# Three F32R products in place of one F32 product in the down-projections of a GNN and expert-FFN kernel

## The chip, the core and the metric

The kernel runs on one core of a Trainium2 chip. A core has five engines that work at the same time, each with a queue of its own that it takes in order: TensorE (PE, with its weight loads shown apart as PEld), VectorE (DVE), ScalarE (ACT), GpSimd (POOL) and SyncE (SP, which here only starts transfers). Matrix products are written to PSUM, which has eight banks of 512 float32 columns on 128 partitions; VectorE and ScalarE read them from there. The metric is the device time of one execution in microseconds (us).

## The reference, cut to what matters

1250 rows of 1024 features pass through four residual layers: a graph attention layer, a wide feed-forward layer with random "rails", a graph convolution, and a mixture of experts. All of it is float32. The change lies in the last layer, whose hidden width is 256:

```python
def geglu(x, w1, w2, w3):
    return jax.nn.gelu(x @ w1, approximate=False) * (x @ w2) @ w3
...
shared = geglu(xf, w1s, w2s, w3s)
idx = jnp.argmax(xf @ Wg, axis=-1)
for e in range(8):
    y = geglu(xf, W1[e], W2[e], W3[e])
    final = final + jnp.where((idx == e)[:, None], y, 0.0)
return x + shared + final
```

The down-projection is the product with w3: [rows, 256] by [256, 1024], once for all rows (shared) and once for each expert on its own rows.

## The kernel before, in words

The first 2460 us of the execution (attention, the wide layer as a blocked fast matrix product, and the graph convolution) hold no edit. The graph convolution ends with a gather (`gather`, L1088 to L1092): counts in F32R times rows that were split into a rounded part and the rest, both F32R, two matmuls each in place of one F32 matmul.

The last layer begins with `hidden` (L1158) for the shared projection: for each half f of the 256 hidden columns and each of three chunks of rows, two groups of eight matmuls (L1166) into the PSUM tiles pab0 and pab1, then a gelu on ScalarE (L1171) and a product on VectorE (L1172). Beside it POOL sends out the row numbers of each expert and gathers the first expert's rows.

Then the shared down-projection: ten tiles t of 125 rows, each with four F32 products (two f, two halves g of the 1024 outputs, L1280), two adds into X on VectorE (L1286) and a write of the tile to base_d by SP (L1287). During the last four tiles, `turn_rows(0)` transposes the first expert's gathered rows on PE (L1269), copied out in turn by VectorE and ScalarE (L1272). After it SP writes all tiles of X to the output (L1289).

Then eight experts, each with room for 224 rows (CAP), in two parts of 128 and 96. `hidden` computes four groups of sixteen matmul rows, and after each group takes one of the four turns of `turn_rows(e + 1)`, the transposes for the next expert. The down-projection has, for each part s and half g, two F32 products into po6 (L1302) and an add on VectorE (L1305) to rows that were gathered from base_d (`rows_of`, L1255); when both halves are done, POOL scatters the part's rows to the output (L1306).

PSUM is shared out so: pool ab has pab0 and pab1 twice (four banks), tps has two banks for transposes, ops6 has po6 twice. w12, w3t, xgT and hid are each held twice, xg and base three times.

The order on each engine's queue and the moment at which a buffer is reused are settled when the program is built: the builder takes instructions by their place in the program and by durations that it estimates, so that loads and gathers can stand far ahead of their place in the text. Each engine then waits on semaphores for what it needs. An F32 matmul in the program appears as two matmul rows in the profile, an F32R matmul as one.

Of the kernel before, what the change touches and what calls it, by code (L numbers as in the profile page):

```python
# [102 lines left out]
def gnn_ffn_kernel(ctx, tc, x, src, dst, gat_w, a_l, a_r, maker, up, cproj,  # L103
# [543 lines left out]
    with nullcontext(ctx) as tail:  # L647
        low = tail.enter_context(tc.tile_pool(name="lowp", bufs=1)).tile([P, T * D], F32, name="low")
# [383 lines left out]
        def weights3(w3t, c):  # L1032
            nc.sync.dma_start(w3t, c.rearrange("(k p) o -> p k o", p=P))
            return w3t
# [116 lines left out]
    with back_end:  # L1151
        hsp = back_end.enter_context(tc.tile_pool(name="hsp", bufs=1))
        hs, w3sh = hsp.tile([P, 2, N], F32, name="hs"), weights3(hsp.tile([P, 2, D], F32, name="w3s"), w3s)
        gp = back_end.enter_context(tc.tile_pool(name="gp", bufs=3))
        with tc.tile_pool(name="ab", bufs=2, space=PSUM) as abp, tc.tile_pool(name="tps", bufs=2, space=PSUM) as tps, \
                tc.tile_pool(name="ops6", bufs=2, space=PSUM) as ops:

            def hidden(dst, w12, rhs, cols, then=None, turns=()):  # L1158
                turns = iter(turns)
                for f in range(2):  # L1160
                    for n0, nn in cols:
# [10 lines left out]
                        nc.vector.tensor_tensor(dst[:, f, n0:n0 + nn], ps[1][:, :nn], g[:, :nn], op=ALU.mult)  # L1172
# [72 lines left out]
            hidden(hs, w12s, xT5, NCH, then=places)  # L1245
# [3 lines left out]
            with tc.tile_pool(name="w12", bufs=2, side="right") as w12p, tc.tile_pool(name="xg", bufs=3) as xgp, \  # L1249
                    tc.tile_pool(name="w3p", bufs=2) as w3p, tc.tile_pool(name="xgT", bufs=2) as xgTp, \  # L1250
                    tc.tile_pool(name="hp", bufs=2) as hp, tc.tile_pool(name="yp", bufs=3, side="right") as yp:
# [6 lines left out]

                xgTs = {}
                out_t = out.rearrange("(t p) d -> t p d", p=R)  # L1260

                def turn_rows(e):
                    xgTs[e] = xgTp.tile([P, KD, CAP], F32, name="xgT")
                    for s, m in parts:
                        xg = rows_of(xn_d, s, m, e * (ROWS // P) + s, "xg")
                        for g in range(2):
# [4 lines left out]
                            eng = nc.scalar.copy if g else nc.vector.tensor_copy  # L1271
                            eng(xgTs[e][:, 4 * g:4 * g + 4, s * P:s * P + m], pt[:, :, :m])  # L1272
# [3 lines left out]
                for t in range(T):  # L1276
                    pos = [abp.tile([P, 512], F32, name=f"pab{g}") for g in range(2)]
                    for f in range(2):
                        for g in range(2):
                            nc.tensor.matmul(pos[g][:R], hs[:, f, t * R:(t + 1) * R], w3sh[:, f, g * 512:(g + 1) * 512],  # L1280
                                             start=(f == 0), stop=(f == 1))
                    if t >= T - 4:
                        next(turns, None)
                    for g in range(2):
                        xs = X[:, t, g * 512:(g + 1) * 512]
                        nc.vector.tensor_tensor(xs, pos[g][:R], xs, op=ALU.add)  # L1286
                    dma(nc.sync, base_d[t * R:(t + 1) * R, :], X[:, t, :])  # L1287
# [3 lines left out]
                for e in range(NE):  # L1291
                    w12 = weights12(w12p.tile([P, 2, KD, F], F32, name="w12"), w1[e], w2[e])
                    w3t = weights3(w3p.tile([P, 2, D], F32, name="w3t"), w3[e])
                    hid = hp.tile([P, 2, CAP], F32, name="hid")
                    hidden(hid, w12, xgTs[e], [(0, CAP)], turns=turn_rows(e + 1) if e + 1 < NE else ())
                    for s, m in parts:
                        i = e * (ROWS // P) + s
                        y = rows_of(base_d, s, m, i, "base")
                        for g in range(2):
                            po = ops.tile([P, 512], F32, name="po6")  # L1300
                            for f in range(2):
                                nc.tensor.matmul(po[:m], hid[:, f, s * P:s * P + m],  # L1302
                                                 w3t[:, f, g * 512:(g + 1) * 512], start=(f == 0), stop=(f == 1))
                            ys = y[:m, g * 512:(g + 1) * 512]
                            nc.vector.tensor_tensor(ys, po[:m], ys, op=ALU.add)  # L1305
# [4 lines left out]
                        tc.add_to_no_dep_group("rows", put.ins)  # L1310

# [80 lines left out]
```

## Time and profile before

| | us |
|---|---|
| median of three runs | 2744.56 (2742.64 to 2751.24) |
| the profiled execution's own time | 2747.47 |
| its span, first to last instruction | 2745.7 |
| PE busy | 2709.5 (99%) |
| DVE busy | 1579.3 (58%) |
| ACT busy | 906.2 (33%) |
| mean granted clock of TensorE | 0.997 |
| shared hidden products | about 2471 to 2540 |
| shared down-projection | about 2540 to 2575 |
| the eight experts | about 2575 to 2740 |

A row of a group gives the line in the kernel, the engine, the operation, the tensors (output, arrow, inputs), the shapes (output, arrow, inputs), the number of instructions, then after the bar the busy time and the mean duration in ns, and after the second bar the idle time ahead of them on that engine and what ended it. A row of the timeline or the chain begins with the start time and the duration, both in us. "PE po L1302 x16" is sixteen matmuls of line 1302 that write the tile po.

### The profile page before, as it was taken

To read this page: it belongs to the slowest core of one execution; us is meant where nothing else is said; L and a number is where in the kernel's file an instruction comes from. 1 tells how busy PE (TensorE), PEld (TensorE's weight loads), DVE (VectorE), ACT (ScalarE), POOL (GpSimd) and SP (SyncE) were. 2 spreads that over 40 slices of the span, in tenths; PEclk is the share of its full clock that TensorE was granted. 3 is DMA by queue.
4 is the path that set the end of the run, shared out by engine and by line. 5 is a ranking of instruction groups with operands and counts; after the bars stand their busy time and mean duration, and the time that the engine had idled before them with its cause. 6 is when DMAs were issued, how large, how long until landed. Compare 5 with 4: busy or idle time off the path is not lost. (4 is left out here: it accounts for less than half of the span.)

```text
span 2745.7 us, 32205 instructions
## 1 busy us (share of the span) xinstructions
PE 2709.5 (99%) x11189; PEld 1893.0 (69%) x11189; DVE 1579.3 (58%) x2708; ACT 906.2 (33%) x1611; POOL 775.8 (28%) x1016
## 2 busy tenths in 40 slices
PE   8999999999999999999999999999999999999998
PEld 6678886676676666766667667666676754675676
DVE  9668988564646556645655556455546765431322
ACT  2333345434434344344343443443432011210000
POOL 2000001243443434434344334343442110112131
PEclk9999999999999999999999999999999999999999
DMA  6336216499999999999999999999998540452784
GB/s 186 92 84 180 71 39 228 164 201 172 210 205 177 227 182 199 199 166 189 190 159 204 179 173 197 166 192 182 143 227 228 169 92 0 87 119 63 270 298 157
DMA packets 269147, 457.74 MB, mean 167 GB/s; under 512 B 53672, under 2 KB 143952, under 8 KB 268593
## 3 DMA queue, kind: packets, MB, share of 16 engines
q0 software_dynamic: 126896, 278.80, 58.7%
q1 hardware_dynamic: 142072, 176.67, 21.4%
q8 instruction: 97, 1.59, 0.2%
q14 instruction: 82, 0.67, 0.1%
HBM read 180.57 MB, written 277.02 MB: 167 GB/s over the span
## 5 line engine op out<-in xcount | busy, mean ns | idle before, releaser
L735 POOL DMA_DIRECT2D acc_d<-low x686 | 589.7, 860 | 914.4 <-ACT low L731 894.1
L731 ACT COPY low<-po 128x626 f32<-128x626 f32 x735 | 501.0, 682 | 952.8 <-PE po L722 891.8
L722 PE MATMUL po<-X,arena 128*128 128x313 f32 x2208 | 619.4, 427 | 0.0
L722 PEld LDWEIGHTS po<-X,arena 128*128 128x128 f32 x2208 | 415.2, 189 | 175.6 <-ACT low L731 16.0
L722 PE MATMUL po<-low,arena 128*128 128x313 f32 x1520 | 429.7, 428 | 0.0
L722 PEld LDWEIGHTS po<-low,arena 128*128 128x128 f32 x1520 | 285.5, 189 | 121.4 <-ACT low L731 11.6
L722 PE MATMUL po<-X,first_w 128*128 128x313 f32 x776 | 222.1, 428 | 1.8 <-DVE X L715 1.8
L722 PE MATMUL po<-X,BZ 128*128 128x313 f32 x720 | 208.5, 433 | 3.6 <-DVE BZ L715 3.6
L722 PEld LDWEIGHTS po<-X,first_w 128*128 128x128 f32 x776 | 145.7, 190 | 64.7 <-ACT low L731 7.6
L722 PE MATMUL po<-low,first_w 128*128 128x313 f32 x624 | 179.5, 429 | 1.0 <-DVE low L715 1.0
L722 PEld LDWEIGHTS po<-X,BZ 128*128 128x128 f32 x720 | 136.9, 192 | 62.6 <-issue 6.1
L722 PEld LDWEIGHTS po<-low,first_w 128*128 128x128 f32 x624 | 117.9, 190 | 50.8 <-ACT low L731 4.4
L227 PE MATMUL pz<-W,xT 128*125 128x256 f32 (+1 forms) x480 | 142.0, 455 | 0.3 <-ACT xT L160 0.3
L715 DVE TENSOR_TENSOR X<-X 128x626 f32<-128x626 f32 x125 | 101.2, 813 | 67.1 <-PE po L722 58.9
L722 PE MATMUL po<-low,BZ 128*128 128x313 f32 x480 | 137.6, 427 | 0.0
L715 DVE TENSOR_TENSOR arena<-arena 128x512 f32<-128x512 f32 x126 | 86.3, 687 | 65.6 <-PE po L722 63.1
L227 PEld LDWEIGHTS pz<-W,xT 128*125 128x125 f32 x480 | 90.0, 190 | 43.8 <-issue 33.8
L715 DVE TENSOR_TENSOR X<-X,low 128x626 f32<-128x626 f32 x105 | 85.3, 816 | 56.2 <-PE po L722 46.0
L722 PEld LDWEIGHTS po<-low,BZ 128*128 128x128 f32 x480 | 90.1, 189 | 38.2 <-ACT low L731 3.7
L715 DVE TENSOR_TENSOR X<-low,X 128x626 f32<-128x626 f32 x101 | 81.7, 813 | 53.3 <-PE po L722 49.0
L707 ACT ACTIVATE X<-pz 128x626 f32<-128x626 f32 (+8 forms) x220 | 101.6, 524 | 17.9 <-PE pz L537 17.9
L715 DVE TENSOR_TENSOR low<-X 128x626 f32<-128x626 f32 x100 | 80.9, 811 | 38.3 <-PE po L722 31.1
(304 smaller groups left out, 3383.6 us busy)
## 6 DMA issues: line engine op xcount, KB each, us to landing
acc_d<-low POOLq DMA_DIRECT2D x735, 313.0 KB, 6.2
arena<-in_cproj SPq DMA_DIRECT2D x148, 256.0 KB
w<-in_w SPq DMA_DIRECT2D x16, 1024.0 KB
BZ<-in_cproj SPq DMA_DIRECT2D x56, 256.0 KB
first_w<-in_cproj SPq DMA_DIRECT2D x52, 256.0 KB
w3t<-in_w SPq DMA_DIRECT2D x8, 1024.0 KB
low<-acc_d SPq DMA_DIRECT2D x19, 313.0 KB
X<-acc_d SPq DMA_DIRECT2D x19, 313.0 KB
```

The lines of the kernel that those rows point to most:

```text
L227: made_z = nc.tensor.matmul(pz, xT[:, k, t * R:(t + 1) * R], W[hs[0] // 2][:, k, i:i + len(hs)], start=(k == 0), stop=(k == KD - 1))
L707: nc.scalar.activation(view(key)[:, :, n0 - n * NQ:n1 - n * NQ], pz[:, 2 * i:2 * i + 2, a + n0 - c0:a + n1 - c0], AF.Gelu)
L715: tt(view(k), *a, op=ALU.add if sign == "+" else ALU.subtract)
L722: nc.tensor.matmul(po[:, o, :NQ], view(x)[:, q, o * P:(o + 1) * P], view(y)[:, q, :], start=(i == q == 0), stop=(i + 1 == len(pairs) and q ...
L731: nc.scalar.copy(part, po[:, :, :NQ])
L735: sent[:] = [nc.gpsimd.dma_start(out=acc_d[p - 1, i - 1], in_=part, accum_op=ALU.add).ins]
```

## The change

It replaces the F32 products of the experts' down-projection, and those of eight of the ten shared tiles, by three F32R matmuls each. Each operand is split into a top part T of 12 bits and the rest l. The stationary ("fixed") operand keeps T, L = 4096 l and S = l - T/4096; the moving operand keeps T, L = l and S = T - 4096 l. Two matmuls add T T and L L into one bank, the third puts S S into a second bank, and the first bank times (1 + 1/4096) plus the second is the product T T + T l + l T + l l. So each result of 512 columns takes two banks, and VectorE adds it in two instructions (`add_sums`).

The parts are made by ScalarE and VectorE: three instructions for each half of a weight matrix (`parts_moving`), four for each half of the hidden columns (`parts_fixed`). Shared tiles 0 and 1 stay F32 products, and the shared weights are split after each of them. An expert's weights are split during its own hidden products, after the first and second group.

The parts of weights and hidden columns lie in the buffer of `low`, which held the transposed rows of the shared projection; the hidden columns of the shared tiles get buffers of their own. w3t is held once instead of twice and is shared with the shared weights, hid once instead of twice. PSUM keeps eight banks: pairs of banks come two out of three times from pool ab and the third time from pool ops6, which now has one pair (`pair_of_sums`).

In an expert the three products of f=0 run for three of the four (s, g) halves, then the last of the four turns, which moves here from the end of `hidden`, then f=1 half by half with its add, and then the fourth half with both f. The copies of transposed rows all go to ScalarE. The gather of base rows now stands in the text with the add, after the products.

Left out of the diff below: the branch for experts with more than 224 rows, which isn't taken here (it makes its transposed rows anew, since `low` is overwritten).

```diff
@@ -1150,12 +1151,44 @@
-        hs, w3sh = hsp.tile([P, 2, N], F32, name="hs"), weights3(hsp.tile([P, 2, D], F32, name="w3s"), w3s)
-        gp = back_end.enter_context(tc.tile_pool(name="gp", bufs=3))
+        w3p = back_end.enter_context(tc.tile_pool(name="w3p", bufs=1))
+        hs, w3sh = hsp.tile([P, 2, 417], F32, name="hs"), weights3(w3p.tile([P, 2, D], F32, name="w3t"), w3s)
+        gp = back_end.enter_context(tc.tile_pool(name="gp", bufs=2))
-                tc.tile_pool(name="ops6", bufs=2, space=PSUM) as ops:
+                tc.tile_pool(name="ops6", bufs=1, space=PSUM) as ops:
...
+            def parts_moving(top, mix, low_part, x):
+                nc.scalar.activation(top, x, AF.Copy, scale=1.0 - 2.0 ** -13)
+                nc.vector.tensor_tensor(low_part, x, top, op=ALU.subtract)
+                nc.vector.scalar_tensor_tensor(mix, low_part, -4096.0, top, op0=ALU.mult, op1=ALU.add)
+
+            def parts_fixed(top, mix, low_part, x):
+                nc.scalar.activation(top, x, AF.Copy, scale=1.0 - 2.0 ** -13)
+                nc.vector.tensor_tensor(low_part, x, top, op=ALU.subtract)
+                nc.vector.scalar_tensor_tensor(mix, top, -(2.0 ** -12), low_part, op0=ALU.mult, op1=ALU.add)
+                nc.scalar.activation(low_part, low_part, AF.Copy, scale=4096.0)
+
+            pairs = [0]
+
+            def pair_of_sums():
+                pairs[0] += 1
+                if pairs[0] % 3 == 0:
+                    return [ops.tile([P, 512], F32, name=f"po{i}") for i in range(2)]
+                return [abp.tile([P, 512], F32, name=f"pab{i}") for i in range(2)]
+
+            def three_products(po, m, f, fixed, moving):
+                (ft, fs, fl), (mt, ms, ml) = fixed, moving
+                for i, (a, b) in enumerate(((ft, mt), (fl, ml))):
+                    nc.tensor.matmul(po[0][:m], a, b, start=(f == i == 0), stop=(f == i == 1))
+                nc.tensor.matmul(po[1][:m], fs, ms, start=(f == 0), stop=(f == 1))
+
+            def add_sums(dst, po, m):
+                nc.vector.scalar_tensor_tensor(dst, po[0][:m], 1.0 + 2.0 ** -12, dst, op0=ALU.mult, op1=ALU.add)
+                nc.vector.tensor_tensor(dst, po[1][:m], dst, op=ALU.add)
...
@@ -1169,7 +1202,9 @@
                         g = gp.tile([P, 417], F32, name="g")
                         nc.scalar.activation(g[:, :nn], ps[0][:, :nn], AF.Gelu)
-                        nc.vector.tensor_tensor(dst[:, f, n0:n0 + nn], ps[1][:, :nn], g[:, :nn], op=ALU.mult)
+                        h = dst(f, n0, nn)
+                        nc.vector.tensor_tensor(h, ps[1][:, :nn], g[:, :nn], op=ALU.mult)
+                        split(f, n0, nn, h)
...
@@ -1242,13 +1277,19 @@
-            hidden(hs, w12s, xT5, NCH, then=places)
+            HK = 2 * R
+            hsT, hsS, hsL = (hsp.tile([P, 2, N - HK], F32R, name=f"hs{i}") for i in "TSL")
+
+            def split_shared(f, n0, nn, x):
+                c0 = max(n0, HK)
+                parts_fixed(*(v[:, f, c0 - HK:n0 + nn - HK] for v in (hsT, hsS, hsL)), x[:, c0 - n0:])
+
+            hidden(lambda f, n0, nn: gp.tile([P, 417], F32, name="h", bufs=2)[:, :nn] if n0 else hs[:, f],
+                   w12s, xT5, NCH, then=places, split=split_shared)
...
-            with tc.tile_pool(name="w12", bufs=2, side="right") as w12p, tc.tile_pool(name="xg", bufs=3) as xgp, \
-                    tc.tile_pool(name="w3p", bufs=2) as w3p, tc.tile_pool(name="xgT", bufs=2) as xgTp, \
-                    tc.tile_pool(name="hp", bufs=2) as hp, tc.tile_pool(name="yp", bufs=3, side="right") as yp:
+            with tc.tile_pool(name="w12", bufs=2, side="right") as w12p, tc.tile_pool(name="xg", bufs=3) as xgp, tc.tile_pool(name="xgT", bufs=2) as xgTp, tc.tile_pool(name="xgT", bufs=2) as xgTp:
...
+                again = lowp.tile([P, T * D], F32R, name="low")
+                w3T, w3S, w3L = (again[:, i * 2 * D:(i + 1) * 2 * D].rearrange("p (f o) -> p f o", f=2) for i in range(3))
+                hidT, hidS, hidL = (again[:, 6 * D + i * 2 * CAP:][:, :2 * CAP].rearrange("p (f n) -> p f n", f=2)
+                                    for i in range(3))
+                hid = xgp.tile([P, 2, CAP], F32, name="hid", bufs=1)
@@ -1268,22 +1315,32 @@
-                            eng = nc.scalar.copy if g else nc.vector.tensor_copy
-                            eng(xgTs[e][:, 4 * g:4 * g + 4, s * P:s * P + m], pt[:, :, :m])
+                            nc.scalar.copy(xgTs[e][:, 4 * g:4 * g + 4, s * P:s * P + m], pt[:, :, :m])
                             yield
...
                 turns = turn_rows(0)
                 for t in range(T):
-                    pos = [abp.tile([P, 512], F32, name=f"pab{g}") for g in range(2)]
-                    for f in range(2):
+                    if t < 2:
+                        pos = [abp.tile([P, 512], F32, name=f"pab{g}") for g in range(2)]
+                        for f in range(2):
+                            for g in range(2):
+                                nc.tensor.matmul(pos[g][:R], hs[:, f, t * R:(t + 1) * R],
+                                                 w3sh[:, f, g * 512:(g + 1) * 512], start=(f == 0), stop=(f == 1))
                         for g in range(2):
-                            nc.tensor.matmul(pos[g][:R], hs[:, f, t * R:(t + 1) * R], w3sh[:, f, g * 512:(g + 1) * 512],
-                                             start=(f == 0), stop=(f == 1))
+                            xs = X[:, t, g * 512:(g + 1) * 512]
+                            nc.vector.tensor_tensor(xs, pos[g][:R], xs, op=ALU.add)
+                        parts_moving(w3T[:, t], w3S[:, t], w3L[:, t], w3sh[:, t])
+                    else:
+                        at = slice(t * R - HK, (t + 1) * R - HK)
+                        pos = [pair_of_sums() for _ in range(2)]
+                        for f in range(2):
+                            for g in range(2):
+                                ws = [w[:, f, g * 512:(g + 1) * 512] for w in (w3T, w3S, w3L)]
+                                three_products(pos[g], R, f, [h[:, f, at] for h in (hsT, hsS, hsL)], ws)
+                        for g in range(2):
+                            add_sums(X[:, t, g * 512:(g + 1) * 512], pos[g], R)
                     if t >= T - 4:
                         next(turns, None)
-                    for g in range(2):
-                        xs = X[:, t, g * 512:(g + 1) * 512]
-                        nc.vector.tensor_tensor(xs, pos[g][:R], xs, op=ALU.add)
                     dma(nc.sync, base_d[t * R:(t + 1) * R, :], X[:, t, :])
@@ -1291,23 +1348,50 @@
                 for e in range(NE):
                     w12 = weights12(w12p.tile([P, 2, KD, F], F32, name="w12"), w1[e], w2[e])
                     w3t = weights3(w3p.tile([P, 2, D], F32, name="w3t"), w3[e])
-                    hid = hp.tile([P, 2, CAP], F32, name="hid")
-                    hidden(hid, w12, xgTs[e], [(0, CAP)], turns=turn_rows(e + 1) if e + 1 < NE else ())
-                    for s, m in parts:
+                    turns = turn_rows(e + 1) if e + 1 < NE else iter(())
+
+                    def beside():
+                        for i in range(4):
+                            if i < 3:
+                                next(turns, None)
+                            if i < 2:
+                                parts_moving(w3T[:, i], w3S[:, i], w3L[:, i], w3t[:, i])
+                            yield
+
+                    hidden(lambda f, n0, nn: hid[:, f], w12, xgTs[e], [(0, CAP)], turns=beside(),
+                           split=lambda f, n0, nn, x: parts_fixed(hidT[:, f], hidS[:, f], hidL[:, f], x))
+                    halves = [(s, m, g, pair_of_sums()) for s, m in parts for g in range(2)]
+
+                    def multiply(halves, f):
+                        for s, m, g, po in halves:
+                            at, to = slice(s * P, s * P + m), slice(g * 512, (g + 1) * 512)
+                            three_products(po, m, f, [h[:, f, at] for h in (hidT, hidS, hidL)],
+                                           [w[:, f, to] for w in (w3T, w3S, w3L)])
+
+                    ys = {}
+
+                    def add_rows(s, m, g, po):
                         i = e * (ROWS // P) + s
-                        y = rows_of(base_d, s, m, i, "base")
-                        for g in range(2):
-                            po = ops.tile([P, 512], F32, name="po6")
-                            for f in range(2):
-                                nc.tensor.matmul(po[:m], hid[:, f, s * P:s * P + m],
-                                                 w3t[:, f, g * 512:(g + 1) * 512], start=(f == 0), stop=(f == 1))
-                            ys = y[:m, g * 512:(g + 1) * 512]
-                            nc.vector.tensor_tensor(ys, po[:m], ys, op=ALU.add)
+                        if g == 0:
+                            ys[s] = rows_of(base_d, s, m, i, "base")
+                        add_sums(ys[s][:m, g * 512:(g + 1) * 512], po, m)
+                        return g and put_rows(m, i, ys[s])
+
+                    def put_rows(m, i, y):
                         put = nc.gpsimd.indirect_dma_start(
                             out=out, out_offset=bass.IndirectOffsetOnAxis(ap=tok[:m, i:i + 1], axis=0),
                             in_=y[:m], in_offset=None, bounds_check=N - 1, oob_is_err=False)
                         tc.declare_no_dep(put.ins, group="rows", reason="rows of their own")
                         tc.add_to_no_dep_group("rows", put.ins)
+
+                    multiply(halves[:3], 0)
+                    next(turns, None)
+                    for h in halves[:3]:
+                        multiply([h], 1)
+                        add_rows(*h)
+                    multiply(halves[3:], 0)
+                    multiply(halves[3:], 1)
+                    add_rows(*halves[3])
 
         with tc.tile_pool(name="ops7", bufs=2, space=PSUM) as ops:
             def project(w3t, h, t, dst):
```

More of the change, by code (lines that the diff above doesn't have):

```diff
@@ L647, in gnn_ffn_kernel @@
     with nullcontext(ctx) as tail:
-        low = tail.enter_context(tc.tile_pool(name="lowp", bufs=1)).tile([P, T * D], F32, name="low")
+        lowp = tail.enter_context(tc.tile_pool(name="lowp", bufs=1))
+        low = lowp.tile([P, T * D], F32, name="low")
         Hs = low[:R].rearrange("p (t d) -> p t d", d=D)
@@ L1155, in gnn_ffn_kernel @@
         with tc.tile_pool(name="ab", bufs=2, space=PSUM) as abp, tc.tile_pool(name="tps", bufs=2, space=PSUM) as tps, \
-                tc.tile_pool(name="ops6", bufs=2, space=PSUM) as ops:
-            def hidden(dst, w12, rhs, cols, then=None, turns=()):
+                tc.tile_pool(name="ops6", bufs=1, space=PSUM) as ops:
[3 more added lines that the diff above has]
+                nc.vector.scalar_tensor_tensor(mix, low_part, -4096.0, top, op0=ALU.mult, op1=ALU.add)
@@ L1159, in hidden @@
+            def hidden(dst, w12, rhs, cols, then=None, turns=(), split=lambda f, n0, nn, x: None):
                 turns = iter(turns)
@@ L1323, in gnn_ffn_kernel @@
                 with tc.tile_pool(name="lw", bufs=1) as lwp, tc.tile_pool(name="lps", bufs=1, space=PSUM) as lps:
+                    low = lowp.tile([P, T * D], F32, name="low")
+                    xT5 = low[:, :KD * N].rearrange("p (k n) -> p k n", k=KD)
+                    for t in range(T):
+                        row = lwp.tile([R, D], F32, name="row")
+                        nc.sync.dma_start(row, xn_d[t * R:(t + 1) * R, :])
+                        for k in range(KD):
+                            pb = lps.tile([P, R], F32, name="lpb")
+                            nc.tensor.transpose(pb, row[:, k * P:(k + 1) * P], ident[:R, :R])
+                            nc.scalar.copy(xT5[:, k, t * R:(t + 1) * R], pb)
                     for e in range(NE):
```

## The prediction

> **What bounds the kernel now.** I read the page's engine line first, then the busy time by stretch of the two stages that the change touches, the chain that ended last, and then the groups by shape for durations.
>
> ```profile
> PE 2709.5 (99%) x11189; PEld 1893.0 (69%) x11189; DVE 1579.3 (58%) x2708; ACT 906.2 (33%) x1611; POOL 775.8 (28%) x1016
> ...
> 2540.00:2576.00 36.00, 36.00 (x99) 16.64 (x98) 15.29 (x23) 0.80 (x2) 0.92 (x1) 1.00 0.65 212
> 2576.00:2740.00 164.00, 162.76 (x751) 128.62 (x749) 36.93 (x63) 13.44 (x31) 41.41 (x44) 1.00 0.75 256
> ...
> 2630.60 6.89 PE po L1302 x16
> 2637.50 3.03 PE pab L1166 x16
> 2640.53 0.44 PE pt L1269 x4
> ```
>
> The columns of the two stretches are length, then busy time of PE, PEld, DVE, ACT, POOL, then granted clock (1.00), DMA share and GB/s. PE is busy for all 36 us of the shared down-projection and 162.8 of the experts' 164; the chain there is PE row on PE row. So TensorE time saved here comes off the end, and any wait put into its queue goes on. VectorE has room (36.9 of 164), ScalarE more.
>
> ```profile
> L1302 PE MATMUL po<-w3t,hid 128*128 128x512 f32 x64 | 29.0, 595 | 0.0
> L1286 DVE TENSOR_TENSOR X<-pab,X 125x512 f32<-125x512 f32 x20 | 13.8, 691 | 20.7 <-PE pab L1280 20.7
> L1097 DVE SCALAR_TENSOR_TENSOR X<-ph,dis,X 125x1024 f32<-125x1024 f32 x10 | 12.7, 1283 | 56.3 <-PE ph L1091 56.3
> L1074 DVE TENSOR_TENSOR xT<-low,Hr 125x1024 fp32r<-125x1024 f32 x9 | 10.4, 1217 | 1.1 <-ACT Hr L1072 1.1
> L974 ACT ACTIVATE low<-low,dis 125x1024 f32<-125x1024 f32 x7 | 8.0, 1149 | 33.2 <-DVE low L1009 22.3 <-DVE low L1013 11.0
> ...
> 2391.07 0.62 PE L1091 MATMUL ph<-Hr,cs 125*125 125x512 f32 x2
> 2391.30 0.41 PEld L1091 LDWEIGHTS ph<-xT,cs 125*125 125x125 f32 x2
> 2391.53 0.63 PE L1091 MATMUL ph<-xT,cs 125*125 125x512 f32 x2
> ```
>
> A matmul's mean (595 ns) overlaps its neighbours; its price is the distance between starts.
>
> **The change, part by part.**
>
> *Products.* An F32 product of 512 columns is two matmul rows (64 products in the program, 128 rows on L1302). The chain gives 6.89/16 = 0.431 us a row, 0.861 a product. The gather (L1091) already multiplies in F32R, one row each: pairs start 0.46 apart, and from 2391.07 to 2396.65 twelve pairs take 5.58, so 0.2325 a row. Three make 0.698. Saved: 0.164 a product, on 8 shared tiles x 4 = 32 and 8 experts x 8 = 64: 96 x 0.164 = **15.7 us**. The row has 125 stationary columns; expert halves have 128 or 96. Bounds: 0.238 (0.2325 x 128/125, 0.5 us less gain) and 0.19 (the mean load of 128 columns alone, 12 us more). I take 0.2325, the same operation at nearly the same size.
>
> [...]
>
> *Start of the shared stage.* Tiles 0 and 1 stay F32 (6.9 us of PE), and cover the splitting of the shared weights. VectorE has, from the last hidden product on (2539.96): 0.59 product, two ops of 416 columns at about 0.57, four adds of 0.69, and per half of the weights a subtraction (1.22, L1074) and a fused op (1.28, L1097, read from PSUM, the nearest row). That is 0.6 + 1.15 + 2.8 + 5.0 = 9.5, done at 2549.5 at the latest if never idle. PE reaches tile 2 at 2546.6, and needs the last part at 2548.4 (after 8 rows). Wait about **1.1 us**; bounds 0 (splits ahead of adds) and 2.2 (one add more in the way).
>
> *Steady shared tiles.* Four adds per tile where there were two: 0.69 for the plain ones, 0.70 for the fused (half of 1.28 is 0.64, the plain 512-column add 0.69; bounds 0.64 and 0.86, L457's 863 for 625 columns). 2.8 a tile plus hand-overs, against 12 x 0.2325 = 2.79 of PE: VectorE bounds tiles 2 to 5 by a little, later ones have a 0.44 turn on PE beside them. **0.3 us**; bounds 0 and 1.3.
>
> *Experts, one boundary.* Zero is PE's end of the hidden products. f=0 of three halves takes 9 x 0.2325 = 2.09, the turn moved here 0.44 (only moved: 2.53), f=1 ends at 3.23, 3.93, 4.62, the fourth half at 6.02. The new chain for f=1's parts: product at 0.27 (0.39), ScalarE 0.36 (gelu of 224 columns), two VectorE ops of 0.37 (L1172's 391 is the bound above), ScalarE 0.36: ready at 2.3. The f=0 products and the turn hide it by 0.2; without them PE would stand 2.3 us at each expert. VectorE adds 1.40 a half from 3.43: done at 4.83, 6.23, 7.63, 9.03. The fourth half reuses the first's banks, freed at 4.13 and 4.83, when PE wants them at 4.62 and 5.09: free. The next expert's hidden products want a pair of abp. Every third pair comes from ops, 16 pairs are used before expert 0, so in experts 0, 3 and 6 the abp pair to come free is the third half's, whose first bank goes after its fused add, at 6.93, where PE is there at 6.02: 0.95 x 3 = **2.9 us**, with all of PE's queue behind it. In the others it is the second half's, free at 5.53. Bounds: 0, and all seven boundaries waiting (6.7).
>
> *Work beside it.* Per expert VectorE goes from 4.8 to 12.8 us (adds 5.6, hidden 0.8, hidden parts 1.5, weight parts 5.0; xgT copies of 1.25 leave), ScalarE from 1.8 to 6.6, under a period of about 19.4 (6.0 of products; 13.4 of four hidden groups at 3.05 and turns). I cost it at nothing, since most of it falls in those 13.4; if VectorE came late to the hidden product, the 2.3 us chain would start late and PE would stand by as much. POOL issues the same 6 gathers and scatters; the scatter of rows goes out 1 to 2 us later per expert. Gathers of base issue at 2683.45 and 2685.84 with about 6 to landing, 4 us before their adds; slack shrinks to about 2. The add waiting on one would hold VectorE.
>
> *w3t in one buffer.* Its load now waits for the previous split instead of running two ahead, on SP's queue:
>
> ```profile
> 2596.64 0.38 SPq L111 DMA_DIRECT2D out_x<-X  x1
> 2598.02 0.41 SPq L1028 DMA_DIRECT2D w<-in_w  x1
> 2599.33 3.50 SPq L1033 DMA_DIRECT2D w3t<-in_w  x1
> ```
>
> Expert 1's is the one in danger: behind the out_x writes, which drain until 2596.6, about 4 earlier now; its issue took 3.50 on SP before; landing by about 2600, wanted by 2602 to be split for products at 2605. While it is late, ScalarE's and VectorE's queues stand with gelu and hidden product behind it. Bounds 0 and 5; I take 0. Later loads have over 10 us.
>
> *Tail.*
>
> ```profile
> 2731.74 7.03 PE L1302 MATMUL po<-w3t,hid 128*128 128x512 f32 x16
> ...
> 2738.80 0.69 DVE L1305 TENSOR_TENSOR base<-po,base 96x512 f32<-96x512 f32 x1 [1.03 <-PE po L1302]
> 2739.77 0.94 POOL L1306 DMA_INDIRECT out_x<-base,tok  x1 [2.41 <-DMA out_x<-base,tok]
> ```
>
> Before, the last add ends 7.75 after zero. After, the first half ends at 2.79 and four halves of adds follow on VectorE: 2.99 + 5.6 = 8.6. Expert 7 gains none of its 1.3 and loses 0.85: **2.2 us**. The scatter behind is the same.
>
> Sum: 15.7 - 1.1 - 0.3 - 2.9 - 2.2 = **9.2 us**. The profiled execution took 2747.47 (span 2745.7), so 2738.3 for it; it lies 2.9 above the median, and from the median 2744.56 the forecast is **2735.4**.
>
> **Rivals.** A difference under 0.3% (8.2 us) counts as none here.
>
> *More waits, of the kinds priced.* For: VectorE's run of adds after each expert (5.6) is as long as PE's products. All seven boundaries (3.8 more) and a late expert 1 (up to 5): gain 0.4 to 5.4, 2739 to 2744. Against: four boundaries have a bank free 0.5 ahead.
>
> *Slower: the next expert's weight split sits ahead of the adds in VectorE's queue.* Its place is settled when the program is built, by estimated durations I don't see; in the code it stands behind the adds. A split placed after the first half's adds can't start until the fourth half's f=0 is done (5.3) and ScalarE's top part (1.15): 6.45 + 2.5 = 8.95, the second half's bank at 9.65, PE waits 3.6. At seven boundaries 25 us, so 15.7 - 1.4 - 2.2 - 25.2 = 13 slower, 2757.7. It decides from 1.74 us of wait per boundary (12.1/7), and beyond the band from 2.9.
>
> *Better: rows near the load's own time, or no boundary waits.* Waits gone: 12.1 to 13.5 gained, 2731 to 2732.5; rows at 0.21 add 6.5, 2725. Nothing in the trace shows such a row.
>
> **How the numbers follow.** Forecast 0.45 (own range 2731 to 2740; a quarter of it inside the band), more waits 0.27, slower 0.18, better 0.10. Faster: 0.34 + 0.10 + 0.02 = 0.46; same: 0.11 + 0.25 = 0.36; slower 0.18. The range runs from 2728, half of the better case, to 2754, the slower case with its wait at six boundaries; about 0.05 lies below and 0.12 above.
>
> **What would show it.** Right: three rows of 512 columns 0.70 apart per product; PE idle ahead of L1166's first hidden row about 1 us in three experts and nearly none in the rest; one wait near 1 us at shared tile 2; the last add about 8.6 after the last hidden product. Wrong: rows at 0.24 or more; PE waiting on a weight part or bank at every boundary; ScalarE waiting on w3t's load in expert 1; a subtraction of 1.2 us between adds in VectorE's order.

## The result, and the profile after

The changed kernel takes 2753.05 us (median; 2744.13 to 2763.54), the kernel before 2744.63 in the same runs (2739.6 to 2755.9). The ratio is 1.0031, with a 95% interval of 1.0021 to 1.0041: slower by about 8.5 us, where 9.2 us less were forecast. The difference is small, but nearly 20 us of savings and losses stand behind it.

The profiled execution of the kernel after took 2746.83 us (span 2745.1), below its median, and the one of before 2747.47 (span 2745.7), above its median. The shared down-projection begins at 2539.7 in the profile of before and at 2531.5 in that of after; in kernels of the later runs that are alike up to there it begins between 2531 and 2543, so that the two spans can't be set against each other whole. I compare by stage, from the start of that projection on.

The page's line of engines, and three stretches of the kernel after (columns as in the prediction: length, busy PE, PEld, DVE, ACT, POOL, granted clock, DMA share, GB/s):

```profile
PE 2695.1 (98%) x11285; PEld 1907.4 (69%) x11285; DVE 1656.3 (60%) x2820; ACT 948.9 (35%) x1689; POOL 805.6 (29%) x1016
...
2531.50:2562.40 30.90, 30.90 (x130) 22.11 (x128) 27.43 (x41) 4.65 (x7) 4.28 (x4) 1.00 0.69 215
2562.40:2605.00 42.60, 25.45 (x131) 21.60 (x129) 11.65 (x19) 8.39 (x17) 8.83 (x10) 0.76 0.93 326
2605.00:2728.00 123.00, 122.75 (x649) 112.60 (x650) 78.50 (x118) 38.35 (x73) 60.61 (x33) 1.00 0.75 241
```

PE's busy time fell by 14.4 us. It is busy throughout the shared projection, which now takes 30.9 us, and from expert 1 on. In between, in expert 0, it is busy for 25.45 of 42.6 us. Its waits from 2500 on (engine, tile and line; who ended the wait; us in total, times, longest), and then ScalarE's for the weight:

```profile
PE pt L1316 <- DMA xg<-xn_d,row_of: 8.6, 2, 8.3
PE pab L1184 <- ACT low L1163: 8.3, 1, 8.3
PE pab L1199 <- DVE base L1188: 0.2, 1, 0.2
```

```profile
ACT low L1163 <- DMA w3t<-in_w: 24.0, 2, 16.8
```

Two waits of 8.3 us are nearly the whole idle time. The first is for gathered rows that are to be transposed: the builder has put 28 transposes for later experts ahead of expert 0's down-projection here (2575.76 to 2588.90), where in the kernel before it put four. The second, behind it, is for the split of expert 0's third weight (L1163 makes its top part), which had waited 16.8 us for the load. The chain has the same place:

```profile
2573.40 0.31 SPq L111
2573.77 11.28 DMA out_x<-X
2585.13 10.96 DMA w3t<-in_w
2596.11 1.06 ACT low L1163
2597.22 0.79 PE pab L1184
```

The load left SP's queue at 2585.13, behind the last writes of X to the output, and took 10.96 us to land. In the kernel before, SP started the loads of experts 0 and 1 together, ahead of all writes of the shared stage, into two buffers. SP's timeline of before:

```profile
2539.99 0.89 SPq L1033 DMA_DIRECT2D w3t<-in_w  x2
2544.04 0.33 SPq L110 DMA_DIRECT2D base_d<-X  x1
```

The stages, read from the first matmul row of each in the timeline, in us (the last column is the run "thin", below: the changed kernel with hardly any bytes written to the output here, and with expert 0's load issued 39 us sooner):

| | before | after | thin |
|---|---|---|---|
| shared down-projection | 35.9 | 30.9 | 30.9 |
| experts 0 and 1 | 41.2 | 60.6 | 39.5 |
| experts 2 to 6 | 102.9 | 95.9 | 96.7 |
| expert 7 to the end | 26.1 | 26.3 | 26.3 |
| sum | 206.0 | 213.6 | 193.4 |

So the arithmetic brings 12 us in the first and third rows, and experts 0 and 1 give 19.4 back. Of these 60.6 us, 16.6 are the two waits; another part is the clock, which was granted at 0.50 from 2582 to 2597.2, where PE was busy for 1.94 us (0.76 on the mean of this stretch; more on it at the end).

### The profile page after: what moved, and what is told of

Same layout as the page of the kernel before. It is cut to its first block, busy times and chain, and to the rows that moved or that the text cites. A ratio compares the mean times of both kernels' runs of the same rounds, so it can differ in the third digit from the quotient of the medians.

```text
span 2745.1 us, 32625 instructions
## 1 busy us (share of the span) xinstructions
PE 2695.1 (98%) x11285; PEld 1907.4 (69%) x11285; DVE 1656.3 (60%) x2820; ACT 948.9 (35%) x1689; POOL 805.6 (29%) x1016
## 3 DMA queue, kind: packets, MB, share of 16 engines
q1 hardware_dynamic: 142072, 176.67, 21.3%
```

## Experiments

My theory after this profile: with one buffer, the load of expert 0 can't be started before the shared weight is split, and then stands in SP's queue behind all writes of the shared stage; placed earlier, it costs nothing (the queue). The rival: the sixteen transfer engines have no room for it between 2570 and 2620, wherever it stands (the bytes). In slices of ten us the share was 0.88, 1.03 and 1.05 from 2570 to 2600 after, and 0.96, 1.02, 1.03 and 1.04 from 2580 to 2620 before. A second rival is that the new arithmetic itself is slower. Medians below stand beside the kernel before in the same runs, 2743.9 to 2746.6.

**Expert 0's load earlier, still one buffer.**

```diff
                         parts_moving(w3T[:, t], w3S[:, t], w3L[:, t], w3sh[:, t])
+                        if t == 1:
+                            w3_first = weights3(w3p.tile([P, 2, D], F32, name="w3t"), w3[0])
...
-                    w3t = weights3(w3p.tile([P, 2, D], F32, name="w3t"), w3[e])
+                    w3t = weights3(w3p.tile([P, 2, D], F32, name="w3t"), w3[e]) if e else w3_first
```

> The changed kernel, with one edit: the load of expert 0's w3 is issued right after the shared weights are split (after shared tile 1), ahead of the other writes on SP, into the same single buffer. Queue theory: the 18.5 us in which PE stood before expert 0's products came from this load standing behind 19 writes of out_x on SP. Then the load lands by about 2550, the gap and PE's waits for gathered rows inside it vanish, and expert 0 takes about 19.5 us instead of 42.6: 2733 to 2737, a ratio of about 0.9965 to before; expert 1's load, still behind the writes, may leave a wait of 0 to 5 us there. Rival, late gathers: PE's 8.3 us wait for gathered rows stays by itself when the weights are early: about 2743. Rival, transfer engines full: the load is late wherever it stands, no change against the changed kernel (2753).

2746.25, ratio 1.0006 (0.9994 to 1.0018). The wait for the weight is gone, and some 7 us of the loss with it, but not the forecast gain. Other waits came, PE's:

```profile
PE pab L1199 <- DVE base L1188: 4.2, 2, 4.0
PE pt L1316 <- DMA xg<-xn_d,row_of: 3.1, 1, 3.1
PE pab L1184 <- DVE base L1188: 2.0, 1, 2.0
```

All are gathers that landed late, or adds that wait for one (the add at 2582.27 stood 4.04 us for its base rows). The queue is a part of it, not the whole.

**Two buffers for the third weight again**, with the new arithmetic. To make room, base has two buffers instead of three, and g and h one each.

```diff
-        w3p = back_end.enter_context(tc.tile_pool(name="w3p", bufs=1))
+        w3p = back_end.enter_context(tc.tile_pool(name="w3p", bufs=2))
```

> The changed kernel with w3t in two buffers (paid for with one buffer less for base, g and h), so that expert 0's w3 is loaded ahead of the shared stage and expert 1's after the split of the shared weights. Queue theory: no wait for w3 in any expert but perhaps expert 1 (its load stands behind the out_x writes, wanted near 2596): 2732 to 2736, ratio 0.9955 to 0.997. If the two buffers of base are too few, VectorE's adds wait for gathers at each expert and PE behind them, some 1 us an expert: 2740 to 2744. Rival, late gathers: 2743.

2754.4, ratio 1.0034 (1.0021 to 1.0047): as slow as the change. Expert 0's load was now started at 2462; those of experts 1 and 2 stood behind the writes (2588.79 and 2592.35), and the chain shows what the second of them, 1 MB, takes there:

```profile
2592.35 19.15 DMA w3t<-in_w
```

**The buffer alone, with the old arithmetic**: the kernel before with one buffer for w3t, shared with the shared weight.

```diff
+        w3p = back_end.enter_context(tc.tile_pool(name="w3p", bufs=1))
-        hs, w3sh = hsp.tile([P, 2, N], F32, name="hs"), weights3(hsp.tile([P, 2, D], F32, name="w3s"), w3s)
+        hs, w3sh = hsp.tile([P, 2, N], F32, name="hs"), weights3(w3p.tile([P, 2, D], F32, name="w3t"), w3s)
```

> The kernel before, its arithmetic untouched, with only one edit: w3t in one buffer that is shared with the shared weights. Queue theory: expert 0's load now goes out behind the out_x writes at about 2597 and lands near 2607, where PE wants it at 2589: a wait of 16 to 20 us ahead of expert 0's products, then a few rows at half the clock: 2761 to 2766. Rival, the new work on VectorE and ScalarE is what made the change slower: this kernel has none of it, 2744 to 2748.

2760.62, ratio 1.0047 (1.0030 to 1.0065). The one buffer costs 13 to 15 us without a single new product. The new arithmetic isn't needed for the loss, so the second rival falls. But the wait that I expected, 16 to 20 us for expert 0's load, isn't there. The builder put expert 1's hidden products ahead of expert 0's down-projection, which covers most of the late load (issued at 2598.47), and PE's waits are mainly for gathered rows:

```profile
PE pt L1270 <- DMA xg<-xn_d,row_of: 5.9, 2, 4.0
PE po L1303 <- DMA w3t<-in_w: 0.9, 1, 0.9
```

From the start of the shared down-projection to the end this execution takes 215.8 us, 9.8 more than before; 6.8 of them are these waits.

**Each tile's output write beside its base write**, so that nothing is left to drain when the experts begin.

```diff
-                for t in range(T):
                     dma(nc.sync, out_t[t], X[:, t, :])
```

(The write moves into the loop of the shared tiles.)

> The changed kernel with each tile's out_x write placed right behind its base_d write, so that the writes spread over the shared stage; expert 0's w3 load still comes after all of them, in one buffer. Queue theory: SP reaches the load at about 2565 instead of 2585, it lands at 2574 to 2580 and PE wants it at 2578: a wait of 0 to 5 us, 2735 to 2741. Rival, transfer engines full: the same bytes go in the same stretch, the wait stays over 10 us and the time above 2746.

2751.02, ratio 1.0026 (1.0013 to 1.0039). The share is now 0.91 to 0.95 in every ten us from 2540 to 2590; the load still stands behind all writes, but leaves SP at 2578.23 in place of 2585.13, and ScalarE waits 3.2 us for it in place of 16.8. PE still waits 8.1 us for an add that lacks its base rows and 7.0 for xg. The queue theory as I had put it falls here: the load comes sooner, and the same bytes cost the same.

**Without the output's writes.** Every row of the output is written again later, by the scatter of its expert or in the branch for full experts, so these ten writes (5 MB) can go. They were taken from the kernel after, from the kernel before, from the one with the early load and from the one with two buffers:

```diff
-                for t in range(T):
-                    dma(nc.sync, out_t[t], X[:, t, :])
```

> The kernel after without the ten writes of the shared result into the output (the rows that each expert scatters later overwrite all of them in this run, as no row is left for the late branch), so 5 MB less to move between 2540 and 2590; one buffer for the third weight as in the change. Theory (the transfer engines are full from about 2570 to 2620, and the weight load that the one buffer moved into that stretch waits there behind these writes): the load of expert 0 is issued by about 2566, its wait falls from 16.8 us to under 2, the shares of 2580 to 2620 fall under 0.9, and the time is 2733 to 2739, some 14 to 20 below the kernel after. Rival (the one buffer costs by its order alone, whatever else is moved): 2744 to 2752. Rival (the new arithmetic itself is slower): above 2750.

> The kernel before without the same ten writes. Its TensorE did not wait in this stretch, so both theories expect the time of before, 2743 to 2747; if it falls under 2741 the writes cost the kernel before something too, and what the run beside it shows is not owed to the new buffer alone.

> The kernel after without the ten writes, and with expert 0's third weight loaded right after the shared weight's parts are made, ahead of the writes of the base rows. Theory: both waits of expert 0 are gone, 2731 to 2737, at most 3 us below the kernel that only lacks the writes. Rival (expert 1 and 2 wait for gathers all the same): 2738 to 2744.

> The kernel with two buffers for the third weight and two for the gathered base rows (one each for the two helpers g and h to make room), without the ten writes: 1 MB more lies in the idle stretch before 2540. Theory: the stretch from the shared stage through expert 2 has 6 MB less to move than in the kernel after, and the time is 2731 to 2737. Rival (the single g and h, or two base buffers, cost by themselves): above 2740.

| | median | ratio to before |
|---|---|---|
| after, without the writes | 2731.92 | 0.9952 (0.9939 to 0.9966) |
| before, without the writes | 2745.02 | 1.0009 (0.9995 to 1.0022) |
| after, early load, without | 2733.91 | 0.9963 (0.9950 to 0.9977) |
| after, two buffers, without | 2730.12 | 0.9959 (0.9942 to 0.9975) |

The changed kernel wins some 13 us over before as soon as 5 MB less have to move, with its one buffer as it is; the kernel before gains nothing by the same edit. But the load isn't late any more: with the writes gone, the builder put expert 0's load at 2542.64 by itself, where it stood at 2585.13 in the kernel after:

```profile
2542.64 0.40 SPq L1034 DMA_DIRECT2D w3t<-in_w  x1
```

Early load (2546.30 in its run) and second buffer add nothing that can be told apart, and this place of the load is a likely reason, not shown as such: no run here has the load late and the bytes gone. The shares from 2580 to 2620 are 1.05, 0.79, 0.95 and 0.80 in the first of the four, not all under 0.9 as expected. Its waits of PE from 2520 on:

```profile
PE pab L1184 <- DVE base L1188: 0.3, 1, 0.3
PE pab L1185 <- DVE base L1189: 0.3, 1, 0.3
PE pab L1199 <- DVE base L1188: 0.3, 1, 0.3
```

**More bytes, old arithmetic.** The dose the other way: the kernel before, and the ten writes once more into a spare array.

```diff
+    more_d = dram.tile([N, D], F32, name="more_d")
...
+                for t in range(T):
+                    dma(nc.sync, more_d[t * R:(t + 1) * R, :], X[:, t, :])
```

> The kernel before with 5 MB more to move: after the ten writes into the output the same rows are written once more into a spare array that nothing reads. Theory (the engines are all but full from 2570 to 2620, with cover of some 10 us at most in the kernel before): later gathers and the weights of expert 2 come late, 2749 to 2762. Rival (the writes stand behind the other work in their queue and use what is left over): 2743 to 2747.

2766.53, ratio 1.0068 (1.0048 to 1.0088). 5 MB less bring the kernel before nothing, 5 MB more cost it 19 to 20 us, in one wait of PE:

```profile
PE pab L1167 <- DMA w<-in_w: 20.9, 1, 20.9
```

By these two runs the kernel before stood at the edge of what this stretch can move. The wait is for weights that SP issued behind the writes, at 2617.78 in place of 2598.02, and that landed in 17.68 us, so queue and bytes both act in it.

**One buffer, old arithmetic, without the writes.** The edits of two runs above together.

> The kernel before with one buffer for the third weight, shared with the shared projection, and without the ten writes into the output. Theory (the one buffer costs only because its loads meet these writes): the 15 us that it lost with the writes come back, 2743 to 2748. Rival (the one buffer costs by itself): 2752 to 2761.

2745.16, ratio 0.9999 (0.9984 to 1.0014). What the one buffer cost comes back whole. The single buffer wasn't slow by itself here; it was slow beside these writes (2760.62).

**Both early loads, all writes kept**: w3t in two buffers, and the loads of experts 0 and 1 ahead of the base writes, about where they were before. In the first of the two runs base has two buffers and xg three, in the second xg two and base three; g and h have one each in both.

```diff
+                            w3_first = [weights3(w3p.tile([P, 2, D], F32, name="w3t"), w3[i]) for i in range(2)]
...
+                    w3t = weights3(w3p.tile([P, 2, D], F32, name="w3t"), w3[e]) if e > 1 else w3_first[e]
```

> The kernel with two buffers for the third weight (two for the base rows, one each for g and h, to make room), and the loads of experts 0 and 1 both put ahead of the writes of the base rows, about where the kernel before had them; all writes kept. Theory (the change lost because it moved these loads behind and beside the writes): 2731 to 2739, much as without the writes, and no wait for a load of the third weight. Rival (the stretch is too full for the shorter experts wherever the loads stand, and the gathers are late all the same): 2742 to 2752.

> The kernel with both early loads and all writes kept, as in the run both_early, but with three buffers for the gathered base rows and two for the rows that are transposed (there it was two and three). In both_early the gather of expert 1's base rows waited for the scatter that freed one of two buffers, and TensorE stood 16.0 us. Theory (that stall belonged to the two base buffers and hid the worth of the early loads): no wait over 2 us there, 2732 to 2740. Rival (the stretch is too full for the shorter experts wherever the loads stand): 2744 to 2754, with the waits at gathers of either kind.

2755.47, ratio 1.0036 (1.0023 to 1.0050), and 2753.30, ratio 1.0029 (1.0012 to 1.0047). The two loads are started at 2463 and 2543 (second run; 2540 for both in the kernel before), and the time does not come back. PE's waits of the first run, then of the second:

```profile
PE po L1184 <- DVE base L1188: 16.0, 1, 16.0
PE pt L1316 <- DMA xg<-xn_d,row_of: 3.4, 1, 3.4
```

```profile
PE pt L1316 <- DMA xg<-xn_d,row_of: 7.9, 2, 4.7
PE pab L1199 <- DVE base L1188: 5.3, 2, 5.1
PE pab L1184 <- DVE base L1188: 1.2, 1, 1.2
```

This speaks for the bytes, but not cleanly: in both runs the scatters of expert 0 stand in POOL's queue behind gathers for later rows until 2610.80 and 2613.79, and one kind of gather has a buffer less. With the writes gone, two base buffers cost nothing (2730.12 above); beside them they may.

**Bytes or order.** A write to the output could also cost by its order, if the first scatter into it had to wait for it; in the kernel after that scatter, at 2604.59, waited 14.5 us for an add. The last three runs part the two. "spare" moves the same bytes into a spare array, "thin" keeps the writes into the output, cut to 64 of 1024 columns, and "spare_early" adds the early load to spare.

```diff
-                    dma(nc.sync, out_t[t], X[:, t, :])
+                    dma(nc.sync, more_d[t * R:(t + 1) * R, :], X[:, t, :])
```

and for thin

```diff
-                    dma(nc.sync, out_t[t], X[:, t, :])
+                    nc.sync.dma_start(out_t[t][:, :64], X[:, t, :64])
```

> The kernel after with the ten writes kept in number, size and place in their queue, but going into a spare array instead of the output (the experts' scatters fill the output in this run). The 5 MB are moved as before; what goes is the rule that the first scatter into the output must wait for them. Theory A (the transfer engines are full): as the kernel after, 2746 to 2755, with the gathers landing late again. Theory B (the scatters of expert 0 wait for the writes into the same array, the base buffers come free late, and the gathers behind them in the queue are late for that): 2731 to 2738 if the load of expert 0 also has time, at most 2744 with its wait of 16.8 us left.

> The kernel after with the ten writes into the output cut to 64 of 1024 columns (0.3 of 5 MB; the scatters overwrite all rows in this run). The waiting of the scatters for them stays, the bytes go. Theory A (full engines): as without the writes, 2730 to 2737. Theory B (the waiting itself): the writes now end by about 2575, so it cannot wait long; B expects the same, and this run alone tells only whether the number of issues matters, in which case 2740 or more.

> As spare, with expert 0's third weight loaded ahead of the writes of the base rows (as in the run early_w3, which stood at 2746 with waits for base rows and for xg of 2 to 4 us each). Theory A: 2744 to 2750, as early_w3. Theory B: the waits for base rows are gone, 2732 to 2738.

spare: 2751.85, ratio 1.0028 (1.0013 to 1.0042). thin: 2730.58, ratio 0.9944 (0.9926 to 0.9961). spare_early: 2743.62, ratio 0.9994 (0.9982 to 1.0007), not to be told from early_w3. The order that the writes could impose is worth nothing that can be seen: without it, spare takes as long as the kernel after (2753.05). The same two stretches in spare and then in thin:

```profile
2580.00:2590.00 10.00, 1.18 (x10) 1.03 (x10) 0.00 (x0) 1.28 (x4) 1.69 (x2) 0.74 1.03 410
2590.00:2600.00 10.00, 3.99 (x13) 2.62 (x12) 2.54 (x3) 2.00 (x2) 0.92 (x1) 0.50 1.05 366
```

```profile
2580.00:2590.00 10.00, 9.52 (x49) 7.59 (x48) 7.60 (x12) 3.83 (x7) 3.64 (x3) 1.00 1.05 335
2590.00:2600.00 10.00, 10.00 (x58) 9.78 (x57) 4.17 (x7) 2.17 (x7) 6.25 (x4) 1.00 0.77 255
```

In thin the share is 1.05 in one slice and 0.77 in the next; in spare it is 1.03 and 1.05, and PE is busy for 1.18 and 3.99 us of ten. But thin and spare differ in more than the bytes: SP issues expert 0's load at 2586.74 in spare. In thin and in spare_early it issues it at nearly the same time:

```profile
2546.28 0.40 SPq L1034 DMA_DIRECT2D w3t<-in_w  x1
```

```profile
2546.73 0.39 SPq L1035 DMA_DIRECT2D w3t<-in_w  x1
```

So the load's place and the bytes can be parted. From spare to spare_early the bytes stay and the load moves: 8.2 us. From spare_early to thin the load stays and the bytes go: 13.0 us. Other runs agree: 6.8 us from after to early_w3, and 12.3 from early_w3 to the run with the early load and without the writes. With the load out of the way, what is left in spare_early is a wait for gathers:

```profile
PE pt L1317 <- DMA xg<-xn_d,row_of: 8.6, 2, 7.5
```

The bytes don't act alone in these 13 us. In spare_early the builder has put 28 transposes for later experts ahead of expert 1's down-projection (from 2604.41), and the waits fall among them; in thin they stand between the groups of hidden products. The full engines and this order aren't parted by any run.

In thin gathers of xg land 4.7 us after their issue (median, 2560 to 2625), where they take 9.1 in the kernel after and 7.6 in spare: in these runs POOL's gathers were slower beside SP's full writes. In the kernel before, with such writes too, they took 5.5.

## Why the prediction was wrong

*Failed: "w3t in one buffer".* The step that decides was costed at 0, with bounds 0 and 5. I looked at expert 1's load, because it was the one that stood behind the writes in the trace of before, and said that later loads had over 10 us. The load in danger was expert 0's: the one buffer holds the shared weight until it is split, and the builder then put the load behind all writes. PE waited 8.3 us behind it, and moved ahead of the writes the load gives back 7 to 8 us (6.8 and 8.2 by medians), above my upper bound of 5. With the late gathers it makes up the second row of the table of stages, 19.4 us more than before in two experts. The sign that I had named for a wrong forecast, ScalarE waiting on w3t's load, is there in both: 16.8 us in expert 0, and 7.1 in expert 1, which no wait of PE follows. Nor is it only a matter of one load being late. I worked out a place in a queue and a landing time from the trace of before, in which the stretch had just room enough, and did not ask whether the engines could take 1 or 2 MB more there. The profile that I had gave the share of whole stages (0.65 and 0.75); in slices of ten us it reads 0.96 to 1.04 from 2580 to 2620, and that was to be seen.

*Missing: the gathers.* I wrote that the slack of base rows shrinks to about 2 us and that "the add waiting on one would hold VectorE", and gave it no price. With the load out of the way (early_w3) this is what remains, 4.0 and 2.0 of PE's waits, and for xg 3.1. Neither rival had it: "more waits" held a late expert 1, up to 5; "slower" rested on VectorE's order, which did not go that way (in the kernel after, the last add of expert 2 starts at 2642.81 and the first subtraction for expert 3 at 2643.41). The slower sign came, by a mechanism that I had priced at nothing.

*Right: the products.* Three rows are 0.70 apart as forecast, in the chain of the kernel after:

```profile
2693.36 0.47 PE pab L1184 x2
2693.83 0.23 PE pab L1185
2694.06 0.47 PE pab L1184 x2
```

So the 15.7 us of PE time are close to what was saved: 32 shared products give 5.0 (35.9 to 30.9; 5.2 by 0.164 each), and the period of an expert falls by 1.20, from 20.57 to 19.37 (experts 3 to 6; 19.4 forecast). A row of 512 columns with a weight load of its own (144 rows and 144 loads of L1184 and L1185 from 2605 to 2728) takes 0.233 us here, 0.70 for three, close to the 0.2325 of the gather.

*Too high: VectorE's waits.* Start of the shared stage 1.1, steady tiles 0.3, three boundaries 2.9: 4.3 forecast. In thin, where nothing else disturbs, PE's waits from 2520 to the end are 0.3, 0.3 and 0.2. The mis-sized term is the add in a queue. I priced each at 0.69 to 0.70; queued, they start 0.60 apart from the second on. VectorE's timeline of thin, last expert, whose first row of the down-projection starts at 2713.91 (zero, as at 2731.74 in the tail of before):

```profile
2717.02 0.69 DVE L1188 SCALAR_TENSOR_TENSOR base<-po,base 128x512 f32<-128x512 f32 x1 [1.02 <-PE po L1184]
2717.72 0.69 DVE L1188 SCALAR_TENSOR_TENSOR base<-pab,base 128x512 f32<-128x512 f32 x1
2718.33 0.68 DVE L1189 TENSOR_TENSOR base<-po,base 128x512 f32<-128x512 f32 x1
2718.93 0.68 DVE L1189 TENSOR_TENSOR base<-pab,base 128x512 f32<-128x512 f32 x1
2719.53 0.68 DVE L1188 SCALAR_TENSOR_TENSOR base<-pab,base 96x512 f32<-96x512 f32 x1
...
2721.32 0.68 DVE L1189 TENSOR_TENSOR base<-po,base 96x512 f32<-96x512 f32 x1
```

The third half's fused add ends 6.30 after zero. In expert 6, with the turn before it, it ends at 2701.80, 6.44 after its zero (2695.36), where 6.93 was forecast, and PE waits 0.3 for it, not 0.95. The last add ends 8.09 after zero (8.6 forecast, 7.75 before). So the tail is 0.3 us longer than before, not 0.85.

*The sum, mended.* 15.7 less 0.8 of waits, 1.3 that expert 7 doesn't gain and 0.3 of tail is 13.3 us. thin gives 2743.85 - 2730.58 = 13.3. That the two agree to a tenth is luck: the stages of the two profiles give 12.6 (206.0 - 193.4), and the interval of the ratio allows 10.7 to 20.3. What was forecast for the arithmetic was too little by 4; what was left out was the transfers, 21.3 us between thin and spare (2751.85 - 2730.58): 8.2 for the load's place, 13.0 for the bytes with what the builder changes for them.

*Open.* How much of the 13.0 is room on the transfer engines, and how much the order in which the builder put transposes and gathers while these bytes were there. Nor is it settled whether the changed kernel would gain with all writes kept, two buffers for w3t and no other buffer given up, which was not tried.

A kernel that beats both is the change without the redundant writes: 2731.92 us, 13.7 below the kernel before.

## What to carry to other kernels

A change that gives up a buffer can move a transfer in time (here expert 0's load, from 2539.99 to 2585.13): look at the share of the transfer engines in fine slices where it will land, not at the mean of a stage, and ask what else lands there; where several slices in a row already read about 1.0, as in the kernel before from 2580 to 2620 (0.96 to 1.04), don't rely on a cover worked out from the trace before: mine did not hold here. A shorter compute stage leaves the same bytes less time (here 30.9 us in place of 35.9, and 19.37 an expert in place of 20.57), so a change that saves TensorE time next to a full stretch should be planned together with the bytes. Look for writes that something later overwrites: here 5 MB of them were free before the change, and were worth 21 us after it, 7 to 8 of which came from the load that moved forward with them. So look up again, after such an edit, when the loads are issued, before putting the gain down to the bytes.

## What the runs showed of the hardware

Where the share of the transfer engines read about 1.0, a load of 1 MB landed in 10.96 us in the kernel after (expert 0's; 1.03 and 1.05 from 2580 to 2600), another in 19.15 with two buffers (expert 2's; 0.99, 1.05 and 1.06 from 2590 to 2620). One issue of such a load on SP's queue took 10.18 us in the kernel before with 5 MB more (1.04 from 2620 to 2640); without them the median of the eight was 0.37 and the longest 3.50. SP's timeline of the kernel before with 5 MB more:

```profile
2617.78 0.55 SPq L1029 DMA_DIRECT2D w<-in_w  x1
2618.38 2.07 SPq L1030 DMA_DIRECT2D w<-in_w  x1
2620.55 10.18 SPq L1034 DMA_DIRECT2D w3t<-in_w  x1
```

In the kernel after TensorE paid twice for its long wait. PE stood from 2578.71 to 2597.2 but for eight transposes (1.94 us); the granted clock was 1.00 until 2580 and 0.50 from 2582 to 2597.2, and PE's first rows behind it, of the same 512 columns, start 0.4 to 0.7 us apart until 2601.07, from where they are 0.23 apart (the granted clock is 0.52 from 2597.20 to 2601.05 and 1.00 behind it):

```profile
2597.22 0.79 PE L1184 MATMUL pab<-low 128*128 128x512 f32 x1 [8.32 <-ACT low L1163]
2597.81 0.63 PE L1184 MATMUL po<-low 128*128 128x512 f32 x1
...
2601.07 0.40 PE L1185 MATMUL pab<-low 128*128 128x512 f32 x1
2601.30 0.40 PE L1185 MATMUL po<-low 128*128 128x512 f32 x1
```

That expert's 24 rows take 7.7 us (2597.22 to 2604.96), at 0.2325 each they would take 5.6: 2 us more. The granted clock was 1.00 again 3.85 us after the first of them began.
